# One row of attention steps for two batches: where values, sums and copies stand at its start, its middle and its end

## The chip, the cores and the metric

The kernel runs on one core of a Trainium2 chip. The metric is the device time of one launch in microseconds (us). A run's time is compared as a median over runs. One further execution of the kernel was recorded by the hardware profiler; all spans, waits and durations below come from that one execution.

## The reference: what is computed

The input x is 2 batches of 256 channels on a 56 x 56 grid, so 3136 tokens of 256 features for each batch, all in float32. Three layers follow one another:

```python
x = _L0_conv_ref(x, ...)                      # 8 groups, no softmax: f = theta^T phi / n, y = f g
t = _to_tokens(x)                             # (2, 3136, 256)
t = t + _L1_attn_ref(_ln_t(t), W_attn, W_proj)
t = t + _L1_ffn_ref(_ln_t(t), gate_w, gate_b, W1, b1, W2, b2)
x = _from_tokens(t, x)
```

The attention has 4 heads of 64 features and a causal mask:

```python
att = jnp.einsum('bhqd,bhkd->bhqk', q, k) * scale
att = jax.nn.softmax(jnp.where(causal, att, jnp.finfo(att.dtype).min), axis=-1)
y = jnp.einsum('bhqk,bhkd->bhqd', att, v)
return y.transpose(0, 2, 1, 3).reshape(B, T, C) @ W_proj
```

The last layer is a gated one: a token's two best of 8 experts (256 to 512 to 256 features, with an exact Gelu between), weighted by their softmax probabilities.

## The kernel before, in words

**Stages.** Up to about 89 us the first layer is folded into one 256 x 256 matrix a batch and applied. From 89 to about 850 us the kernel does the attention of batch 0 and then of batch 1, with the normalisation, the q, k and v products, the output projection and the routing to experts worked in between. From 850 us to the end it does the experts: 102 blocks of 128 token slots, each through `hidden` (first layer, `ht`, L1541) and `outputs` (second layer, `yp`, L1560), and adds the two expert results of each token.

**A step of attention.** `attend` (L708) is called once for each batch. It makes a list `steps`: for each block `i` of W = 448 queries (NB = 7 blocks) and each pair of heads `hp` (NH = 2 pairs), one step for every key chunk `j` of 128 keys. Within a block, whole chunks come first, and the last ones alternate with the cut ones, those that the causal mask cuts. A step has two halves:

- `scores` (L734): TensorE (PE) multiplies keys by queries into a PSUM tile `sc` (pool `psc`, two buffers), as 64x64 quarters of the array; ScalarE (ACT) takes the exponential into a tile `st` of the pool `fst` (five buffers, L753); on cut chunks VectorE (DVE) multiplies by the mask (L755). Then VectorE adds `st` into the running row `acc` (pool `fs`, two buffers): the first step of a block copies `st` into `acc` (L763), all others add (L767).
- `values` (L772): PE multiplies `st` by the values `v` into `yp` (pool `py`, one PSUM buffer). After a block's last step ScalarE copies `yp` into the buffer that `acc` was in (L796) and GpSimd (POOL) adds the two halves of it into `qT` (L797).

The main loop (L853 to L873) goes over `n`: it does `scores(n)` and `values(n - LAG)` with LAG = 3. So at the start of each call there are three scores without values, and at its end three values without scores. The order in which the code is written is the order of every engine's queue: PE, VectorE, POOL, SP and ScalarE are all under a manual schedule, and nothing moves the instructions afterwards.

**Visits.** Two steps after a block and head pair ends (BEHIND = 2) the loop calls `visit(i, hp)` (L2041) and then `sum_rows`. A visit puts other PE work between the steps: the pieces that `ahead` (L2000) names, which are transposes of normalised tokens (`xs`, PE `xp`, L600, then a ScalarE copy `px`, L606), query and key products (`qks`, L614) and value products (`vs`, L629) of the next segment of tokens, and up to two pieces of the output projection (`products`, PE `pp`, L683). POOL normalises the tokens (L585) as `xs` asks for them, one tile in advance. At the change of batch, the transposes of batch 1's first segment lie in the visit of (block 6, pair 0), and its q, k and v products and the next transposes in the visit of (block 6, pair 1), the last of batch 0's call. For batch 0 the same pieces stand ahead of the first call. In a visit PSUM tiles are taken in turn from pool `m` (two) and pool `psc` (two) by `bank` (L524) with `ring`; outside it, only from pool `m`.

`sum_rows` (L800) has PE sum `acc` over its partitions (`sp`, L809), ScalarE copy the line out (L814) and SP send it through DRAM. `invert` (four steps later) takes the reciprocal and has it spread over partitions (`rb`), `scale` (six more) multiplies the block of `qT` by it on VectorE (L841), and `hand_on` (two more) tells the projection that the block is ready. The value copy goes into `acc`'s buffer because `sum_rows` comes ahead of the block's last `values`, whose step is one later than the visit.

**The end of attention.** The last visit, of (batch 1, block 6, pair 1), loads ScalarE's table for Gelu with a one-element activation (L2045) and does one projection, `pp`. Then come the sums, the last values and, in `experts` (L1436), the register load of the experts of the first three blocks (`experts_of`, L1500), the transposes of the first block's tokens (`inputs`, PE `tp`, L1518, and a ScalarE copy `xT`, L1522), the copy of its first-layer weights by VectorE (`w`, L1529), and `hidden`. `between` (L2055) runs once a step: it issues loads of second-layer weights during the last rows and pulls other work (statistics, routing) from a queue.

The lines that make the order around the change:

```python
                LAG, BEHIND = 3, 2
                for n in range(len(steps) + LAG):
                    if BEHIND < n <= len(steps) + BEHIND and steps[n - 1 - BEHIND][4]:
                        visit(i, hp)
                        sum_rows(hp, i)
```

Of the kernel before, what the change touches and what calls it, by code (L numbers as in the profile page):

```python
# [28 lines left out]
def conv_attn_moe_kernel(  # L29
# [482 lines left out]
    def layer1(nm, general):  # L512

        with ExitStack() as whole:
# [192 lines left out]

            def attend(  # L708
                b, qT, kT, v, fst, fs, psc, py, visit, between, clock, later, finished
            ):  # L710

                steps, firsts = [], {}
                for i in range(NB):
# [13 lines left out]
                    for hp in range(NH):  # L729
                        for r, j in enumerate(order):  # L730
                            steps.append((i, hp, j, r == 0, r == len(order) - 1, order))
                sts, accs, yps = {}, {}, {}

                def scores(n):  # L734
                    i, hp, j, first, last, order = steps[n]
# [25 lines left out]
                    if first:  # L761
                        acc = fs.tile([P, 2, W], F32, tag="acc", name=f"acc_{sn}")
                        nc.vector.tensor_copy(acc, st)  # L763
                        accs[hp, i] = acc
                    else:
                        acc = accs[hp, i]
                        nc.vector.tensor_tensor(  # L767
                            acc[:k, :, c0:], acc[:k, :, c0:], st[:k, :, c0:], ALU.add
                        )
                    sts[n] = st  # L770

                def values(n):  # L772
                    i, hp, j, first, last, order = steps[n]
# [4 lines left out]
                    if first:  # L778
                        yps[hp, i] = py.tile([P, 2, 512], F32, tag="y", name=f"yp_{sn}")
                    yp = yps[hp, i]  # L780
# [11 lines left out]
                    if last:  # L792

                        yh = qT[:, hp, i * W : (i + 1) * W]
                        both = accs.pop((hp, i))
                        nc.scalar.copy(both, yp[:, :, :W])  # L796
                        nc.gpsimd.tensor_tensor(yh, both[:, 0], both[:, 1], ALU.add)  # L797
                        del yps[hp, i]

                def sum_rows(hp, i):  # L800
# [3 lines left out]
                    acc = accs[hp, i]  # L804
# [18 lines left out]
                    later.append((clock[0] + 4, invert, hp, i, yh))  # L823

                def invert(hp, i, yh):
# [12 lines left out]
                    later.append((clock[0] + 6, lambda hp, i, yh: scale(hp, i, yh, rb), hp, i, yh))  # L838

                def scale(hp, i, yh, rb):  # L840
                    nc.vector.tensor_tensor(yh, yh, rb, ALU.mult)  # L841
                    later.append((clock[0] + 2, hand_on, hp, i, yh))

                def hand_on(hp, i, yh):
                    finished[hp] = (i + 1) * W

                def due(now):
                    while later and (now is None or later[0][0] <= now):
                        _, task, hp, i, yh = later.pop(0)
                        task(hp, i, yh)  # L850
                        later.sort(key=lambda e: e[0])

                ends = {i: max(n for n, s in enumerate(steps) if s[0] == i) for i in range(NB)}  # L853
                LAG, BEHIND = 3, 2
                for n in range(len(steps) + LAG):
                    if BEHIND < n <= len(steps) + BEHIND and steps[n - 1 - BEHIND][4]:
                        i, hp = steps[n - 1 - BEHIND][:2]
                        visit(i, hp)
                        sum_rows(hp, i)
                    if n < len(steps):  # L860
                        i = steps[n][0]
                        between(i, ends[i] - n, (steps[n][2] + 1) * P > i * W + 1)

                    late = n >= LAG and steps[n - LAG][3]
# [7 lines left out]
                    if late:  # L872
                        values(n - LAG)  # L873
                return due
# [560 lines left out]

            def experts(w1s, w2s, b2s, ex, es, ps6, between, need, written, settle, decide):  # L1436
# [63 lines left out]
                def experts_of(r):  # L1500

                    b = 0 if (r + 1) * GB <= FULL0 else 1
                    s = r * GB - known[b][0]
                    return nc.values_load_multi_w_load_instructions(
                        eblks[b][0:1, s : s + GB],
# [821 lines left out]
```

## Time and profile before

| | |
|---|---|
| runs: median (lowest to highest) of 3 | 1278.05 us (1276.01 to 1281.41) |
| the profiled execution, its own time | 1279.51 us |
| its span in the trace | 1277.8 us |
| mean granted TensorE clock | 0.998 |
| L767, VectorE's adds into `acc` | x372, 373.1 us busy |
| L753, ScalarE's exponentials | x400, 330.4 us busy |
| L785 and L745, PE's values and scores | 337.3 and 335.9 us busy |
| L763, VectorE's copies into `acc` | x28, 18.0 us busy |

The table's lower half is from the profile's list of the costliest groups. Busy time is the time in which an engine had an instruction of the group in flight. The idle time in front of a row, and the instruction named with an arrow, say what the engine waited for last. In a timeline, a row is a run of like instructions: its start from the start of the span, its length, the engine, the line, the operation, and how many. Rows of PE overlap by a little, since matmuls are pipelined and their ends are modelled, so distances are best taken from start to start. "The chain" is the path of work that ended last, followed back from the last instruction.

### The profile page before, as it was taken

To read this page: it belongs to the slowest core of one execution; us is meant where nothing else is said; L and a number is where in the kernel's file an instruction comes from. 1 tells how busy PE (TensorE), PEld (TensorE's weight loads), DVE (VectorE), ACT (ScalarE), POOL (GpSimd) and SP (SyncE) were. 2 spreads that over 40 slices of the span, in tenths; PEclk is the share of its full clock that TensorE was granted. 3 is DMA by queue.
4 is the path that set the end of the run, shared out by engine and by line. 5 is a ranking of instruction groups with operands and counts; after the bars stand their busy time and mean duration, and the time that the engine had idled before them with its cause. 6 is when DMAs were issued, how large, how long until landed. Compare 5 with 4: busy or idle time off the path is not lost.

```text
span 1277.8 us, 28550 instructions
## 1 busy us (share of the span) xinstructions
PE 1251.2 (98%) x10809; PEld 816.4 (64%) x10809; DVE 786.6 (62%) x1711; ACT 613.2 (48%) x1237; POOL 357.9 (28%) x319
## 2 busy tenths in 40 slices
PE   8999999999999999999999999999999999999998
PEld 8875545444444444545544443469889899899996
DVE  2673567666777745576677878785744443455664
ACT  0255555565556555455555655553333333344432
POOL 1103230000002204221102666100256112666651
PEclk9999999999999999999999999999999999999999
DMA  9995001000000000100000123541334333466654
GB/s 312 357 346 177 24 18 32 25 9 25 9 17 10 25 1 17 35 16 9 9 9 22 66 71 100 199 137 65 100 130 150 105 113 101 142 198 199 212 160 126
DMA packets 111073, 123.87 MB, mean 97 GB/s; under 512 B 19703, under 2 KB 100840, under 8 KB 110930
## 3 DMA queue, kind: packets, MB, share of 16 engines
q1 hardware_dynamic: 100274, 95.41, 24.2%
q0 software_dynamic: 9840, 25.67, 6.0%
q8 instruction: 89, 1.46, 0.5%
q10 hardware_dynamic: 816, 0.88, 0.2%
q14 instruction: 54, 0.44, 0.1%
HBM read 62.06 MB, written 61.05 MB: 96 GB/s over the span
## 4 chain that ended last, share of the span: by engine, by line
PE 93%; DVE 3%; issue 1%; ACT 1%; another core or an unknown queue 0%; DVEq 0%; DMA 0%; ACTq 0%
PE yp_f L785 20%; PE sc_f L745 20%; PE ht_f L1541 14%; PE yp_f L1560 13%; PE qk_f L614 7%; PE v_f L629 4%; PE pp_f L683 3%; PE cp L410 3%; PE gram L317 2%; PE tp_f L1518 2%; DVE acc_f L767 1%; PE sp_f L809 1%; PE yo_f L1787 1%; PE xp_f L600 1%; ACT st_f L753 1%
## 5 line engine op out<-in xcount | busy, mean ns | idle before, releaser
L767 DVE TENSOR_TENSOR acc_f<-acc_f,st_f 128x896 f32<-128x896 f32 (+5 forms) x372 | 373.1, 1003 | 127.2 <-ACT st_f L753 117.4
L753 ACT ACTIVATE st_f<-sc_f 128x896 f32<-128x896 f32 (+5 forms) x400 | 330.4, 838 | 203.2 <-PE sc_f L745 182.8
L785 PE MATMUL yp_f<-st_f,v_f 64*64 64x448 f32 (+6 forms) x3184 | 337.3, 500 | 3.8 <-DVE st_f L755 2.0
L745 PE MATMUL sc_f<-qT_f,kT_f 64*64 64x448 f32 (+6 forms) x3184 | 335.9, 499 | 1.5 <-ACT st_f L753 1.4
L1550 ACT ACTIVATE g_f<-ht_f,b1b 128x128 f32<-128x128 f32 x408 | 116.6, 372 | 234.0 <-PE ht_f L1541 116.0
L745 PEld LDWEIGHTS sc_f<-qT_f,kT_f 64*64 64x64 f32 x3184 | 118.9, 133 | 154.6 <-issue 139.2
L785 PEld LDWEIGHTS yp_f<-st_f,v_f 64*64 64x64 f32 x3184 | 116.5, 133 | 156.7 <-issue 126.7
L1541 PE MATMUL ht_f<-xT_f,w_f 128*128 128x128 f32 x1632 | 203.2, 276 | 7.4 <-issue 6.3
L1541 PEld LDWEIGHTS ht_f<-xT_f,w_f 128*128 128x128 f32 x1632 | 197.5, 192 | 14.4 <-issue 9.1
L1420 POOL DMA_INDIRECT x_slots<-xr_f,idx x100 | 120.5, 1205 | 146.6 <-DMA y_slots<-ys_f 62.9
L797 POOL TENSOR_TENSOR qT_f<-acc_f 128x448 f32<-128x448 f32 x28 | 32.0, 1143 | 450.1 <-ACT acc_f L796 450.1
L1529 DVE COPY w_f<-w1s_f 128x1024 f32 x102 | 72.4, 711 | 95.5 <-PE ht_f L1541 32.1
L585 POOL TENSOR_SCALAR xn_f<-t 128x256 f32<-128x256 f32 (+1 forms) x50 | 84.8, 1704 | 156.9 <-PE xp_f L600 68.6
L1581 POOL DMA_INDIRECT y_tokens<-ys_f,to_f x57 | 58.9, 1034 | 127.8 <-DVE ys_f L1570 107.7
L614 PE MATMUL qk_f<-px_f,wat 128*128 128x512 f32 (+2 forms) x224 | 88.2, 546 | 0.6 <-ACT px_f L606 0.6
L1570 DVE TENSOR_TENSOR ys_f<-yp_f,kT_f 128x128 f32<-128x128 f32 x102 | 29.5, 289 | 88.3 <-PE yp_f L1560 62.5
L614 PEld LDWEIGHTS qk_f<-px_f,wat 128*128 128x128 f32 x224 | 40.6, 190 | 45.7 <-issue 41.0
L1560 PE MATMUL yp_f<-px_f,g_f 128*128 x204 | 61.6, 383 | 1.3 <-issue 1.3
L1560 PE MATMUL yp_f<-kT_f,g_f 128*128 x204 | 61.1, 381 | 0.0
L1560 PE MATMUL yp_f<-v_f,g_f 128*128 x204 | 61.0, 381 | 0.0
L755 DVE TENSOR_TENSOR st_f<-st_f,keep 128x256 f32<-128x256 f32 (+1 forms) x112 | 44.9, 401 | 26.2 <-ACT st_f L753 25.6
L1560 PE MATMUL yp_f<-w2s_f,g_f 128*128 x204 | 60.7, 379 | 0.0
(287 smaller groups left out, 1224.8 us busy)
## 6 DMA issues: line engine op xcount, KB each, us to landing
x_slots<-fill SPq DMA_DIRECT2D x1, 8190.0 KB
xb_f<-x_slots SPq DMA_DIRECT2D x60, 130.0 KB
x_slots<-fill SPq DMA_DIRECT2D x1, 7296.0 KB
y_slots<-ys_f SPq DMA_DIRECT2D x57, 128.0 KB
kept<-t SPq DMA_DIRECT2D x2, 3200.0 KB
x<-in_x_dram SPq DMA_DIRECT2D x14, 448.0 KB
rb_f<-inverses SPq DMA_DIRECT2D x56, 112.0 KB
y_f<-y_tokens SPq DMA_DIRECT2D x23, 256.0 KB
```

The costliest lines, as they stand in the source:

```text
L585: nc.gpsimd.tensor_scalar(xn[:k, a], ts[b][:k, n + a, :C], ts[b][:k, n + a, MEAN : MEAN + 1], ts[b][:k, n + a, RSTD : RSTD + 1], ALU.subtr ...
L614: nc.tensor.matmul(ps[:, :w], wat[:, c, d0 : d0 + P], px[:, s % 2, c, :w], start=(c == 0), stop=(c == NH - 1),)
L745: nc.tensor.matmul(ps[h : h + HS, a, c0:W], kT[hp][rows, j * P + h : j * P + h + HS], qT[rows, hp, q0 + c0 : q0 + W], start=True, stop=True,)
L753: nc.scalar.activation(st[:k, :, c0:], ps[:k, :, c0:W], AF.Exp, scale=SCALE)
L767: nc.vector.tensor_tensor(acc[:k, :, c0:], acc[:k, :, c0:], st[:k, :, c0:], ALU.add)
L785: nc.tensor.matmul(yp[a * HS : (a + 1) * HS, h // HS, c0:W], v[hp][h : h + HS, j, a, :HS], st[h : h + HS, a, c0:], start=first, stop=bool( ...
L1420: s = nc.gpsimd.indirect_dma_start(out=xds[b], out_offset=bass.IndirectOffsetOnAxis(ap=idxs[b][:kk, k, n : n + 1], axis=0), in_=xr[:kk], i ...
L1529: nc.vector.tensor_copy(w, w1s[:, :, bass.ds(e, 1), :].rearrange("p c e h -> p c (e h)"))
L1541: nc.tensor.matmul(ht[:, k, :], w[:, c, k * P : (k + 1) * P], xT[:, c, :], start=(c == 0), stop=(c == NH - 1),)
L1550: nc.scalar.activation(g[:, k, :], ht[:, k, :], AF.Gelu, bias=b1bs[b][:, k, i : i + 1])
L1560: nc.tensor.matmul(yp[:, :C], g[:, k, :], w2s[k][:, bass.ds(e, 1), :].rearrange("p e d -> p (e d)"), start=(k == 0), stop=(k == KH - 1),)
L1581: s = nc.gpsimd.indirect_dma_start(out=y_tokens, out_offset=bass.IndirectOffsetOnAxis(ap=to[:, n % GB : n % GB + 1], axis=0), in_=ys, in_o ...
```

## The change

1. `attend` is called once. `steps` holds both batches' steps in one list, so the values of batch 0's last three steps alternate with the scores of batch 1's first ones. `open_batch(b)`, called when a batch's first step comes, puts the batch's work into the queue.
2. Visits are kept in a table by step. A first one, (0, -1, 1), at step 2 holds what stood ahead of the first call: batch 0's value products of segment 0 and transposes of segment 1. They come after two scores.
3. At the change of batch, the transposes of batch 1's segment 0 go into the visit of (batch 0, block 5, pair 1); its q, k and v products and half of the next transposes into the visit of (block 6, pair 0), which comes FREED + LAG + 1 = 8 steps after that pair's last step in place of 3; the rest into the visit of (block 6, pair 1), which now lies among batch 1's first steps.
4. The first step of a block makes no copy: its `st` is kept, and the second step adds both into `acc`. Where the second step is cut (block 0), the columns ahead of the cut are copied: four small copies.
5. Where a block's last values come ahead of its sums, their copy goes into a buffer of the exponentials (`both`, from `fst`), since `acc` is still needed. That is so for (batch 0, block 6, pair 0) and for the last block and pair of all.
6. At the end, whole and cut chunks of the last block and pair change places. The last visit is one step earlier. In it, two first blocks of expert tokens are transposed and copied into a part of `qT` (`early_input`), with the Gelu table load ahead. The sums come after all values. The register load for the first experts goes into the visit of (batch 1, block 6, pair 0).

In the order of instructions, apart from this, one load of second-layer weights stands earlier in SP's queue, and six normalisation instructions of batch 1 stand ahead of one add (L797) in POOL's queue. The experts' order is the same after the first two blocks.

The core of the diff:

```diff
-                for i in range(NB):
+                for b, i in ((b, i) for b in range(B) for i in range(NB)):
...
                     for hp in range(NH):
+                        if (b, i, hp) == (B - 1, NB - 1, NH - 1):
+                            for r in range(len(order) - 2 * (nk - len(whole_js)), len(order), 2):
+                                order = order[:r] + [order[r + 1], order[r]] + order[r + 2 :]
...
                     if first:
-                        acc = fs.tile([P, 2, W], F32, tag="acc", name=f"acc_{sn}")
-                        nc.vector.tensor_copy(acc, st)
-                        accs[hp, i] = acc
+                        single[b, hp, i] = st
+                    elif (b, hp, i) in single:
+                        one = single.pop((b, hp, i))
+                        acc = accs[b, hp, i] = fs.tile([P, 2, W], F32, tag="acc", name=f"acc_{sn}")
+                        nc.vector.tensor_tensor(acc[:, :, c0:], one[:, :, c0:], st[:, :, c0:], ALU.add)
+                        if c0:
+                            nc.vector.tensor_copy(acc[:, :, :c0], one[:, :, :c0])
...
-                        both = accs.pop((hp, i))
+                        both = accs[b, hp, i]
+                        if (b, hp, i) not in summed:
+                            both = fst.tile([P, 2, W], F32, tag="st", name=f"both_{sn}")
                         nc.scalar.copy(both, yp[:, :, :W])
...
-                LAG, BEHIND = 3, 2
+                LAG, BEHIND, FREED = 3, 2, 4
+                visits = {BEHIND: (0, -1, NH - 1)}
+                for n, s in enumerate(steps):
+                    if s[5]:
+                        change = s[0] + 1 < B and s[1:3] == (NB - 1, 0)
+                        visits[n + 1 + (FREED + LAG if change else BEHIND)] = s[:3]
+                final = visits.pop(len(steps) + BEHIND)
+                visits[len(steps) + 1] = final
                 for n in range(len(steps) + LAG):
...
+                    if n in visits:
+                        visit(*visits[n])
+                        b, i, hp = visits[n]
+                        if i >= 0 and visits[n] != final:
+                            sum_rows(b, hp, i)
...
+                sum_rows(final[0], final[2], final[1])
                 return due
...
+            def early_input(n, qT):
+
+                tp = bank(f"first_{n}")
+                for c in range(NH):
+                    nc.tensor.transpose(
+                        tp[:, c * P : (c + 1) * P], early_rows[n][:, c * P : (c + 1) * P], ident
+                    )
+                xT = qT[:, :, n * P : (n + 1) * P]
+                nc.scalar.copy(xT, tp[:, : NH * P].rearrange("p (c t) -> p c t", c=NH))
+                early_xT.append(xT)
...
                 def ahead(b, i, hp):
...
+                    if i < 0:
+                        return vs(0), xs(1)
                     if i + 1 < NS:
                         if hp == 0:
                             return qks(i + 1), xs(i + 2)[:1]
-                        return vs(i + 1), xs(i + 2)[1:]
+                        after = projections[b + 1][0](0) if i + 2 == NS and b + 1 < B else []
+                        return vs(i + 1), xs(i + 2)[1:] + after
                     if b + 1 == B:
                         return [], []
                     xs, qks, vs = projections[b + 1]
                     if hp == 0:
-                        return [], xs(0)
-                    return qks(0) + vs(0), xs(1)
+                        return qks(0) + vs(0), xs(1)[:1]
+                    return [], xs(1)[1:]
...
+                    last = b + 1 == B and i + 1 == NB
+                    if last and hp == 0:
+                        assert ranked[0]
+                        early_ids.extend(experts_of(0))
+                    if last and hp + 1 == NH:
                         nc.scalar.activation(warm, eps5[:1], AF.Gelu)
+                        while len(early_rows) < 2:
+                            pull(every=True)
+                        now = [partial(early_input, n, qT) for n in range(2)]
                     ring.append(0)
```

## The prediction, made before the changed kernel had run

> **What bounds the kernel now.** I read the page's busy list and chain first, to find the engine that sets the end; then busy time by stage, to see where that engine has room left; then what it waits for inside the attention; then its order of time at each place that the change touches.
>
> ```profile
> PE 1251.2 (98%) x10809; PEld 816.4 (64%) x10809; DVE 786.6 (62%) x1711; ACT 613.2 (48%) x1237; POOL 357.9 (28%) x319
> PE 93%; DVE 3%; issue 1%; ACT 1%; another core or an unknown queue 0%; DVEq 0%; DMA 0%; ACTq 0%
> ```
>
> TensorE is busy for 98% of the span and is 93% of the chain that ended last. No other engine comes near, so the change can only win what TensorE loses while it waits. The stage table (start:end, length, then busy time of PE, PEld, DVE, ACT, POOL) says how much that is; the stages are attention of batch 0, attention of batch 1, and the experts:
>
> ```profile
> 89.00:463.00 374.00, 371.63 (x3635) 179.53 (x3638) 244.26 (x370) 215.83 (x327) 61.25 (x42) 1.00 0.13 39
> 463.00:852.00 389.00, 383.81 (x3718) 184.96 (x3711) 274.73 (x507) 217.30 (x327) 118.64 (x82) 1.00 0.17 52
> 852.00:1278.00 426.00, 410.08 (x2794) 378.21 (x2792) 218.48 (x673) 157.82 (x536) 168.06 (x160) 0.99 0.45 139
> ```
>
> PE is idle for 374.00 − 371.63 = 2.4 us and 389.00 − 383.81 = 5.2 us in the two attention stages, 7.6 us together: a ceiling near 0.6% of the kernel, before drains, which count as busy. The granted clock is 1.00, so there is no throttle to win from. What PE waits for between 89 and 852 us (total, times, longest):
>
> ```profile
> PE yp_f L785 <- DVE st_f L755: 2.0, 5, 0.8
> PE yp_f L785 <- ACT acc_f L796: 1.8, 3, 0.6
> PE sc_f L745 <- ACT st_f L753: 1.4, 3, 0.6
> PE ht_f L1541 <- ACT xT_f L1522: 0.8, 1, 0.8
> PE qk_f L614 <- ACT px_f L606: 0.6, 1, 0.6
> PE sp_f L809 <- ACT px_f L606: 0.5, 2, 0.2
> PE sp_f L809 <- DVE acc_f L767: 0.3, 1, 0.3
> ```
>
> These few waits sit at the start of each batch, where scores have no values to alternate with, and at the hand-over to the experts. PE at the batch change (start, length, work, idle before and releaser):
>
> ```profile
> 476.06 0.59 PE L809 MATMUL sp_f<-acc_f,ones 128*32 128x224 f32 x8 [0.24 <-ACT px_f L606]
> 479.45 0.94 PE L745 MATMUL sc_f<-qT_f,kT_f 64*64 64x192 f32 x16 [0.60 <-ACT st_f L753]
> 481.35 0.77 PE L785 MATMUL yp_f<-st_f,v_f 64*64 64x320 f32 x8 [0.21 <-DVE st_f L755]
> 493.20 1.52 PE L785 MATMUL yp_f<-st_f,v_f 64*64 64x448 f32 x16 [0.63 <-ACT acc_f L796]
> ```
>
> and at the end of attention, PE, then DVE, then POOL:
>
> ```profile
> 847.79 0.59 PE L809 MATMUL sp_f<-acc_f,ones 128*32 128x224 f32 x8 [0.27 <-DVE acc_f L767]
> 849.22 0.66 PE L1518 MATMUL tp_f<-ident,xb_f_first 128*128 128x128 f32 x4
> 850.63 2.05 PE L1541 MATMUL ht_f<-xT_f,w_f 128*128 128x128 f32 x16 [0.76 <-ACT xT_f L1522]
> ```
>
> ```profile
> 849.36 1.29 DVE L1529 COPY w_f<-w1s_f 128x1024 f32 x2 [1.28 <-PE yp_f L785]
> ```
>
> ```profile
> 850.38 1.26 POOL L797 TENSOR_TENSOR qT_f<-acc_f 128x448 f32<-128x448 f32 x1 [34.59 <-ACT acc_f L796]
> ```
>
> **What the Trainium skill says.** "TensorE: Matmul & The Clock Gate", section "Step-by-step: what each phase is for": matmuls stay in program order, and the drain of one hides beside the next but not where it stands alone. The trace agrees: where the timeline shows 0.27 us idle ahead of the sums at 847.79, more is lost (the four pp matmuls at 846.37 are 0.94 us of work, and 1.42 pass). I therefore price joints start to start, not by the idle figure. "ScalarE: Activation LUTs", section "What ACT_TABLE_LOAD costs", gives about 1283 ns for the load; the load for Gelu took 1.28 us at 846.63. "Runtime: NRT & Kernel Launch", section "Instruction fetch mechanics", says that instruction refills are mostly hidden, and that a register load is about 200 ns. This trace shows no idle time at the experts' register loads in front of 849.22 and of 852.74, but 7.6 us of "issue" stalls on PE in the experts (6.3 over 12 first-layer and 1.3 over 2 second-layer groups), which nothing else in the profile releases.
>
> **Part 1: the first steps of batch 0.** Now four v blocks, two transposes (xp), four scores, then values and scores by turns. Changed: two scores first, then v and xp, then the rest; no work is added. From the start of v at 99.74 to that of the next qk at 110.89 (both from the chain, in time) is 11.15 us. The work, each at its rate between neighbours (eight records of 64x448 0.75, 320 0.54, 192 0.33, 64 0.11; 16 v records 3.76; eight transposes 0.88): 3.76 + 0.88 + scores 0.75 + 0.54 + 0.33 + 0.11 + values 0.75 + 0.54 + 0.33 and scores of the next half 0.75 + 0.54 = 9.28. Lost: 1.87. It goes because ScalarE's exponentials of the two scores (0.92 + 0.70) and VectorE's masks (0.42 each) now lie beside 4.64 us of v and xp; v only needs transposed input, ready before. Gain **1.8**. ScalarE's queue: the two exponentials stand ahead of eight v copies of 0.27, 1.6 us late at most; with four banks v can go on, so 0.1 is left as a loss.
>
> **Part 2: the batch change.** From 464.32 (qk) to 483.84 (next qk) 19.52 us pass. Work: qk 7.06 + v 3.76 + xp 0.88 + sums 0.52 + last values 0.75 + four scores 1.73 + three values 1.62 + two scores 1.29 = 17.61. Lost 1.91. The visit at 425.06 loses 0.30 more (5.46 us for 5.16). Changed: batch 1's first scores follow batch 0's last in the same loop, so they have values to alternate with; qk and v of batch 1 move forward to the earlier visit, which itself is five steps later, when the overwritten keys are read out. They cost the same 10.82 there, and ScalarE has 4 x 0.585 + 8 x 0.27 = 4.5 us of copies beside it. What is late next: PSUM for values has one buffer, so batch 1's first values wait for ScalarE's copy out of batch 0's last (0.905 us), as they do at every block: waits of 0.58 at 120.20 and 0.63 at 493.20. Here less than two scores stand between, so 0.6 to 0.75 stays. Queued behind that values instruction on PE are all later scores. Gain 2.21 − 0.7 = **1.5**. The value copy moves to an exponentials' buffer (one of five) and is held for copy plus POOL's add, 0.905 + 1.14; the buffer's next turn is five steps on, over 7 us, so nothing. On POOL six normalisation instructions of batch 1 (1.56 each: four took 6.24 us at 392.89) pass ahead of one add at 391.76. POOL is idle for 31.32 us before that add and four of the six wait for nothing on PE, so they run there; two wait for a transpose and make the add up to 3.1 us late. It is needed by a scaling ten steps (15 us) on: nothing; without that cover, 3.1 on VectorE's queue. The two waits of the sums for px (0.24) go as well: the sums' bank no longer is one that px is being copied from.
>
> **Part 3: the end.** From 844.60 (score) to 852.90 (second first-layer group) 8.30 us pass for 6.21 of work: 2.09 lost. Changed: the whole and cut key blocks of the last row swap places, the two first expert blocks are transposed before the last projection, values come before the sums. ScalarE's xT copies and the table load (1.28 + warm 0.20) then lie under 0.94 of pp and 0.75 of values, and the sums wait for no add. Late next, first: VectorE's copy of the first weights (0.69 each; two take 1.29) may start only when the last values are read, as now at 849.36, and only the sums (0.52) cover it: 0.3 stays with the hand-over. Next: the second weights lie over the memory of the new value copy, so they wait for ScalarE 0.905, POOL 1.14 to 1.26, then 0.69 of their own, 2.8 with nothing between, against 0.52 + 0.3 + 1.78 + 0.22 = 2.8 on PE: 0.25 with hand-overs. Behind that waiting copy on VectorE stand the routing operations and later weights, not needed for 2 us. About 0.4 of drains stays. Gain 2.09 − 0.95 = **1.15**. The register load for the first block's experts goes into an earlier visit: no idle now, so nothing; if it shows there, the skill's price is 0.2 a register, two engines: up to 0.4 lost. One load of second-layer weights on SP's queue goes earlier; these land by 856 and are first used at 858.75: nothing, and if late, the 2.7 us of slack is its size.
>
> **Part 4: the copies.** 28 copies of 0.642 (18.0 us, line L763) go from VectorE, and four of 256 elements come, under 0.425 each, which an add of that size takes: 16.3 us off VectorE at 62%. The first exponentials stay in their buffer one step longer, of five: nothing. What of it is PE's? PE's waits for VectorE are the five of L755, 2.0 us. Two are the 0.2 ones of parts 1 and 2. The other three, at 529.91, 660.69 and 765.14, lose 1.01, 0.45 and 0.61 start to start, 2.07 in all. In front of them I find a queue of statistics, scalings by rb and routing work, not a copy, so I give **0.2**; bounds 0 and 2.07.
>
> **Sum.** 1.8 + 1.5 + 1.15 + 0.2 = 4.65, taken as 4.6. The profiled execution took 1279.51 with a span of 1277.8 (1.7 outside); it would take 1274.9, the span 1273.2. It stands 1.5 above the median of the runs, 1278.05, which gives 1273.4, −0.36%. About 0.5% (6.4 us) is what a measurement of this kernel can tell from no change.
>
> **Rivals.**
> A, the relief reaches further: the copies stood in the same VectorE queue all along, so the backlog at the three stalls of batch 1 is shorter by 0.64 a block, and the 2.07 goes whole, with a little of ScalarE's late starts. For: VectorE is 274.73 of 389.00 there. Against: none of the three has a copy in front. 6.7 gained: 1271.4.
> B, new waits take the place of the old: the one values buffer at the batch change and the POOL chain at the end each cost one more us or so. For: both rest on one more hand-over; against: both were counted. 2.3 gained: 1275.7.
> C, slower: instruction supply. The stream of each engine is shifted and the experts' stalls (7.6 us, of no visible cause) depend on where refills meet DMA peaks (share 0.45 there). If they double, −4.6 + 7.6 = +3.0: 1281.1. It decides from 4.6 us of new stalls. Against: the experts' order is the same.
> The change not doing what it says is hardly open: the order of instructions on the five engines shows the moves as told.
>
> **Chances.** Main case 0.50 (1272 to 1275), A 0.27, B 0.14, C 0.09. Faster by over 0.5% needs under 1271.66: more than half of A and a little of the main case, 0.30. Slower by over 0.5% (above 1284.4): the upper part of C, 0.04. The rest, 0.66, lies within. Range: from A with the late ScalarE starts, 1269.0, to B with the register load and drains, and the lower edge of C, 1279.0.
>
> **What would show it.** Right: next qk after the start comes 9.4 us after v plus two scores; no L753 wait at the batch change, one values wait there of 0.6 to 0.75; first-layer group two at about 1.15 + 3.3 us earlier than 852.90; L763 only four times; the three stalls in batch 1 still there. Wrong: those stalls gone (A); a wait over 1 us at the values after the change, or at the second first-layer group (B); "issue" stalls above 7.6 us in the experts (C).

## The result, and the profile after

The changed kernel takes 1275.2 us (median of 10 runs, 1269.95 to 1278.06); the kernel before took 1278.38 us (median of 10, 1274.22 to 1281.56). The ratio of the runs is 0.9963, with a 95% interval of 0.9950 to 0.9976: 0.37% faster, or 4.7 us by the ratio (3.2 by the medians alone). The forecast was 0.36%. The same kernel was measured twice more in the experiments, on two chips: 0.9954 (0.9940 to 0.9969) and 0.9957 (0.9943 to 0.9971).

The profile of the changed kernel, its busy list and chain first:

```profile
PE 1250.1 (98%) x10809; PEld 817.6 (64%) x10809; DVE 771.6 (61%) x1687; ACT 612.8 (48%) x1237; POOL 355.2 (28%) x319
PE 95%; DVE 2%; issue 1%; ACT 1%; DMA 0%; DVEq 0%; SPq 0%; ACTq 0%
```

VectorE has 24 instructions and 15.0 us less (16.3 were forecast). TensorE's busy time is the same within 1.1 us, and its share of the chain rises from 93 to 95%: what changed is when it waits. The stages:

```profile
89.00:463.00 374.00, 372.77 (x3554) 183.17 (x3556) 229.39 (x353) 214.24 (x333) 63.13 (x44) 1.00 0.13 39
463.00:849.00 386.00, 381.79 (x3798) 183.26 (x3790) 274.45 (x500) 218.19 (x322) 113.81 (x80) 1.00 0.17 54
849.00:1275.20 426.20, 410.10 (x2794) 378.48 (x2792) 219.30 (x676) 158.13 (x536) 168.22 (x161) 0.99 0.44 138
```

The second stage is cut at 849 in place of 852, since the second first-layer group begins that much earlier. TensorE's waits up to there:

```profile
PE yp_f L788 <- ACT acc_f L801: 2.3, 4, 0.6
PE yp_f L788 <- DVE st_f L754: 1.5, 3, 0.8
PE qk_f L614 <- ACT px_f L606: 0.6, 1, 0.6
PE sc_f L744 <- ACT st_f L752: 0.6, 1, 0.6
PE ht_f L1573 <- DVE w_f L1561: 0.3, 1, 0.3
```

The two waits on masks of 0.2, the waits of the sums and the 0.8 on `xT` are gone; the waits of values for ScalarE's copy went from three to four. The start of batch 0 on TensorE, before and then changed:

```profile
106.51 0.94 PE L745 MATMUL sc_f<-qT_f,kT_f 64*64 64x192 f32 x16 [0.50 <-ACT st_f L753]
108.44 0.77 PE L785 MATMUL yp_f<-st_f,v_f 64*64 64x320 f32 x8 [0.22 <-DVE st_f L755]
```

```profile
106.36 0.67 PE L744 MATMUL sc_f<-qT_f,kT_f 64*64 64x192 f32 x16
106.86 1.47 PE L788 MATMUL yp_f<-st_f,v_f 64*64 64x448 f32 x16
```

The waits on the exponential and on the mask are gone. The batch change, changed:

```profile
475.88 0.59 PE L815 MATMUL sp_f<-acc_f,ones 128*32 128x224 f32 x8
477.20 0.62 PE L744 MATMUL sc_f<-qT_f,kT_f 64*64 64x192 f32 x16
478.40 1.52 PE L788 MATMUL yp_f<-st_f,v_f 64*64 64x448 f32 x16 [0.59 <-ACT acc_f L801]
490.86 1.52 PE L788 MATMUL yp_f<-st_f,v_f 64*64 64x448 f32 x16 [0.58 <-ACT acc_f L801]
```

The sums and the scores come without a wait; at 478.40 stands the new one, for the single values buffer. The end on TensorE, on VectorE and on POOL:

```profile
844.31 0.66 PE L1471 MATMUL first_f<-ident,xb_f_first 128*128 128x128 f32 x4
846.80 0.58 PE L815 MATMUL sp_f<-acc_f,ones 128*32 128x224 f32 x8
847.67 2.05 PE L1573 MATMUL ht_f<-qT_f,w_f 128*128 128x128 f32 x16 [0.28 <-DVE w_f L1561]
849.86 2.05 PE L1573 MATMUL ht_f<-qT_f,w_f 128*128 128x128 f32 x16
```

```profile
846.92 0.69 DVE L1561 COPY w_f<-w1s_f 128x1024 f32 x1 [0.51 <-PE yp_f L788]
849.11 0.69 DVE L1561 COPY w_f<-w1s_f 128x1024 f32 x1 [1.50 <-POOL qT_f L802]
```

```profile
847.95 1.13 POOL L802 TENSOR_TENSOR qT_f<-both_f 128x448 f32<-128x448 f32 x1 [33.96 <-ACT both_f L801]
```

The first weights are copied once the last values are read, and the first group waits 0.28 for them. The second copy waits for POOL's add, which began when ScalarE's value copy was done.

**Where the time went.** I cut each span at the same five instructions, start to start: *start*, from the first v product or score after q and k to the next q and k; *change*, from there to the q and k products that follow batch 1's first scores; *inside*, from there to the last score but one; *end*, from there to the third first-layer group; *experts*, the rest. (The last score but one is the 64x64 one in the old order of the last row and the full one in the new; ahead of either, the same scores and values are done.)

| kernel | start | change | inside | end | experts |
|---|---|---|---|---|---|
| before | 11.24 | 372.95 | 360.30 | 10.67 | 423.06 |
| changed | 9.59 | 371.60 | 360.79 | 9.71 | 423.23 |
| e1, start undone | 10.74 | 371.61 | 358.20 | 9.71 | 406.97 |
| e2, copies back | 9.59 | 371.60 | 358.68 | 9.71 | 406.91 |
| e3, drained | 9.58 | 372.69 | 358.21 | 9.70 | 407.05 |
| e4, end undone | 9.59 | 371.60 | 358.20 | 10.68 | 407.87 |
| e5, changed again | 9.59 | 371.60 | 358.97 | 9.71 | 417.55 |
| e6, before without copies | 10.74 | 372.40 | 359.68 | 10.67 | 419.07 |
| e9, changed, third | 9.59 | 371.60 | 359.20 | 9.71 | 422.22 |
| e11, register load late | 9.59 | 371.60 | 361.00 | 9.88 | 419.22 |
| e12, value copy in acc | 9.59 | 371.61 | 359.03 | 9.51 | 421.51 |

In e7, e8 and e10 some steps pass these cuts, so they are compared over the longer stretches given with them.

Where a joint is built alike, the first two columns and the fourth repeat to 0.01 us, while whole executions of one kernel differ by several us. So the joints are read from the profiles, and the ratios below only bear out the sum. The changed kernel wins 1.65 at the start, 1.35 at the change and 0.96 at the end: 3.96 us. In this one pair of profiles 0.49 is lost inside and 0.17 in the experts, and the joints begin 0.70 later; the last section looks at how far these three are chance.

### The profile page after: what moved, and what is told of

Same layout as the page of the kernel before. It is cut to its first block, busy times and chain, and to the rows that moved or that the text cites. A ratio compares the mean times of both kernels' runs of the same rounds, so it can differ in the third digit from the quotient of the medians.

```text
span 1275.2 us, 28500 instructions
## 1 busy us (share of the span) xinstructions
PE 1250.1 (98%) x10809; PEld 817.6 (64%) x10809; DVE 771.6 (61%) x1687; ACT 612.8 (48%) x1237; POOL 355.2 (28%) x319
## 4 chain that ended last, share of the span: by engine, by line
PE 95%; DVE 2%; issue 1%; ACT 1%; DMA 0%; DVEq 0%; SPq 0%; ACTq 0%
PE yp_f L788 21%; PE sc_f L744 20%; PE ht_f L1573 14%; PE yp_f L1592 14%; PE qk_f L614 7%; PE v_f L629 4%; PE pp_f L683 4%; PE cp L410 3%; PE gram L317 2%; PE tp_f L1550 2%; PE sp_f L815 1%; DVE acc_f L770 1%; PE xp_f L600 1%; PE yo_f L1819 1%; PE tail_f L1684 0%
## 5 line engine op out<-in xcount | busy, mean ns | idle before, releaser
L752 ACT ACTIVATE st_f<-sc_f 128x896 f32<-128x896 f32 (+6 forms) x400 | 330.4, 838 | 203.4 <-PE sc_f L744 185.5
L770 DVE TENSOR_TENSOR acc_f<-acc_f,st_f 128x896 f32<-128x896 f32 (+6 forms) x344 | 344.3, 1001 | 122.0 <-ACT st_f L752 112.6
L1573 PE MATMUL ht_f<-xT_f,w_f 128*128 128x128 f32 x1600 | 199.5, 276 | 7.8 <-issue 7.6
L1573 PEld LDWEIGHTS ht_f<-xT_f,w_f 128*128 128x128 f32 x1600 | 194.0, 192 | 14.7 <-issue 10.5
```

What stands on the lines that cost most here:

```text
L752: nc.scalar.activation(st[:k, :, c0:], ps[:k, :, c0:W], AF.Exp, scale=SCALE)
L770: nc.vector.tensor_tensor(acc[:k, :, c0:], acc[:k, :, c0:], st[:k, :, c0:], ALU.add)
L1573: nc.tensor.matmul(ht[:, k, :], w[:, c, k * P : (k + 1) * P], xT[:, c, :], start=(c == 0), stop=(c == NH - 1),)
```

## The experiments

Ratios are to the kernel before on the same chip, with 95% intervals. e1 to e4 shared one chip, e5 to e8 another, e9 to e12 a third. The changed kernel itself did not run beside e1 to e4, so what each of these four lost is read from the profiles. Added back to their ratios (3.3, 3.3, 2.9 and 3.4 us faster than before), the losses 1.15, 0.47, 1.09 and 0.97 put the changed kernel 3.8 to 4.4 us ahead on that chip, an estimate with 1.1 to 1.4 us to either side.

**e1: the start undone.**

```diff
-                for piece in keys[2:]:
+                for piece in keys[2:] + vs(0) + xs(1):
-                visits = {BEHIND: (0, -1, NH - 1)}
+                visits = {}
```

> The changed kernel with part 1 alone undone: batch 0's v products and transposes stand ahead of the first score again. Theory (the gain sits in the joints where TensorE waited): from the first of these instructions to the next qk about 11.2 us in place of 9.6, with the waits of 0.5 on an exponential and 0.2 on a mask back; the rest unchanged, so about 1.65 us slower than the changed kernel. Rival (VectorE's relief is what gained): this joint's length does not come back to 11.2, since the copies stay away.

Ratio 0.9974 (0.9965 to 0.9983). The start is 10.74: it lost 1.15 of the 1.65. Neither theory has that: the first wanted all of it back, and the rival is right for the 0.50 that stays away. On TensorE and on VectorE there:

```profile
106.50 0.94 PE L744 MATMUL sc_f<-qT_f,kT_f 64*64 64x192 f32 x16 [0.50 <-ACT st_f L752]
107.25 1.50 PE L788 MATMUL yp_f<-st_f,v_f 64*64 64x448 f32 x16
```

```profile
106.48 1.04 DVE L754 TENSOR_TENSOR st_f<-st_f,keep 128x256 f32<-128x256 f32 x2 [2.45 <-ACT st_f L752]
107.55 0.87 DVE L765 TENSOR_TENSOR acc_f<-st_f,st_f 128x640 f32<-128x640 f32 x1
```

The wait on the exponential is back, the one on the mask is not. VectorE masks the first two chunks one after the other. In the kernel before, a copy stood between these masks:

```profile
106.49 0.70 DVE L755 TENSOR_TENSOR st_f<-st_f,keep 128x256 f32<-128x256 f32 x1 [2.45 <-ACT st_f L753]
107.22 0.84 DVE L763 COPY acc_f<-st_f 128x896 f32<-128x896 f32 x1
107.98 0.41 DVE L755 TENSOR_TENSOR st_f<-st_f,keep 128x256 f32<-128x256 f32 x1
```

So at this start the copy had been on the path, in front of the second mask; the start is 0.50 us shorter without it.

**e2: the copies back.** The first step of a block makes `acc` and copies `st` into it, as before; all else is the changed kernel.

```diff
                     if first:
-                        single[b, hp, i] = st
-                    elif (b, hp, i) in single:
-                        one = single.pop((b, hp, i))
-                        acc = accs[b, hp, i] = fs.tile([P, 2, W], F32, tag="acc", name=f"acc_{sn}")
-                        nc.vector.tensor_tensor(acc[:, :, c0:], one[:, :, c0:], st[:, :, c0:], ALU.add)
-                        if c0:
-                            nc.vector.tensor_copy(acc[:, :, :c0], one[:, :, :c0])
+                        acc = accs[b, hp, i] = fs.tile([P, 2, W], F32, tag="acc", name=f"acc_{sn}")
+                        nc.vector.tensor_copy(acc, st)
```

> The changed kernel with part 4 alone undone: every first exponential is copied into acc again, 28 copies of 0.64 us more on VectorE (about 16 us net). Theory (copies cost nothing on the path): no TensorE wait appears in front of a block's first steps, the joints keep their lengths, and the time is within 0.5 us of the changed kernel. Rival A (the relief shortens VectorE's backlog): 1 to 2 us slower, with longer waits on L754's masks in batch 1 or longer joints.

Ratio 0.9974 (0.9963 to 0.9984). Start, change and end are as in the changed kernel to the hundredth. Inside batch 1 it is 358.68 against 358.20 and 358.21 of e1, e3 and e4 on the same chip: the copies cost 0.47 us there. Of these, 0.18 are lost at the transposes at 636.49; the same 0.18 stand in the kernel before, at 638.31, and in no profile without copies. The rest is in this one profile alone. The long wait on a mask moves little, from 0.83 in e1 to 0.94 here:

```profile
528.09 0.66 PE L783 MATMUL yp_f<-st_f,v_f 64*64 64x256 f32 x8 [0.94 <-DVE st_f L754]
```

The rival's 1 to 2 us is not there.

**e3: the pipeline drained between the batches.**

```diff
+                    if b + 1 < B and i == NB - 1:
+                        steps += [None] * 3
```

The loop skips these three steps.

> The changed kernel with three empty steps between the two batches: the last values of batch 0 and the first scores of batch 1 no longer alternate, while the q, k and v products stay where the change put them. Theory (the interleaving is what part 2 won): waits of 0.6 on an exponential and 0.2 on a mask come back at batch 1's first scores, the values wait of 0.59 goes; 0.9 us slower in all between the two qk landmarks. Rival (what part 2 won is the moved products and the banks): no slower than 0.3 us there.

Ratio 0.9977 (0.9968 to 0.9986). The change is 1.09 longer, of the 1.35 that it had won. TensorE:

```profile
475.31 0.59 PE L817 MATMUL sp_f<-acc_f,ones 128*32 128x224 f32 x8 [0.77 <-DVE acc_f L772]
478.66 0.94 PE L746 MATMUL sc_f<-qT_f,kT_f 64*64 64x192 f32 x16 [0.56 <-ACT st_f L754]
479.42 1.47 PE L790 MATMUL yp_f<-st_f,v_f 64*64 64x448 f32 x16
```

The wait on the exponential is back as expected, and the values wait went. Not expected: the sums wait 0.77 for the last add, since of the work that stood ahead of them in the kernel before only half of the transposes is left; and the mask's 0.2 stays away, as in e1. So the rival, at most 0.3, falls, but that the total comes near the theory's 0.9 is luck in part: start to start the sums lose 0.84 more than in the changed kernel, which the theory had not. The products' new places win nothing by themselves: e6 below, in the old order, takes 372.40 without copies, and e3 takes 372.69.

**e4: the end undone.** The swap of the last row, `early_input` and the later sums are taken out; the register load stays early.

```diff
-                        if (b, i, hp) == (B - 1, NB - 1, NH - 1):
-                            for r in range(len(order) - 2 * (nk - len(whole_js)), len(order), 2):
-                                order = order[:r] + [order[r + 1], order[r]] + order[r + 2 :]
...
-                final = visits.pop(len(steps) + BEHIND)
-                visits[len(steps) + 1] = final
...
-                        now = [partial(early_input, n, qT) for n in range(2)]
```

> The changed kernel with part 3 undone but for the early register load: old order of the last row, last visit and sums ahead of the last values, the first two expert blocks transposed after attention. Theory: the stretch from the last full score to the third first-layer group is about 1.0 us longer, with 0.76 of wait on xT and 0.27 on the last add back; 1.0 us slower. Rival (the table load and xT copies were hidden anyway, the end's gain is chance): within 0.3 us.

Ratio 0.9973 (0.9965 to 0.9982). The end is 10.68, 0.97 longer, and both waits are back in the list:

```profile
PE ht_f L1567 <- ACT xT_f L1548: 0.8, 1, 0.8
PE sp_f L812 <- DVE acc_f L767: 0.3, 1, 0.3
```

The kernel before, with the late register load, has 10.67: in the old order the early load wins nothing.

**e5 and e9: the changed kernel again.** No edit.

> The changed kernel unaltered, beside the kernel before on the same chip as the three that follow. In the runs e1 to e4 the experts had no issue stalls and the late exponentials of the first two profiles were absent. Theory (three joints 4.0 us, VectorE's relief some 0.3 inside batch 1): 4.3 us faster than before, ratio about 0.9966. Rival (the first profiles' difference of 2.6 is the true one): 0.998.

> The changed kernel once more, as the measure for the three runs beside it on one chip. Up to the experts it should repeat its landmarks: 9.59 us from the first score to the next qk, 371.60 to batch 1's qk, 9.71 from the last full score to the third first-layer group. Theory (the experts' stalls belong to the chip and the execution, not to the order of the kernel): the experts' length may be anywhere between 405 and 423 us. Rival (the experts' length follows the kernel's order): near the 417.6 of e5.

e5 is at 0.9954 (0.9940 to 0.9969), e9 at 0.9957 (0.9943 to 0.9971). The joints are the same to the hundredth. 0.998, which the rival of e5 gave, lies outside both intervals; the theory's 0.9966 lies inside, near their upper ends. The experts took 417.55 and 422.22 with the same instructions in the same order, so the rival of e9, that their length follows the order, falls.

**e6: the kernel before without the copies.** Part 4 alone, put into the old loop in the same form (the reverse of e2's diff).

> The kernel before with part 4 alone: no copies of the first exponentials. e1 showed the old start at 10.74 us in place of 11.24 when the copies are gone. Theory now: the copy stands in front of the masks in VectorE's queue at each batch's first steps, so each of the two starts is 0.5 shorter, with the 0.2 waits on L755 gone, and the inside of batch 1 gains 0.3 to 0.5: 1.3 us faster than before in all, ratio 0.999. Rival (copies are wholly off the path): both starts keep their lengths of 11.24 and 19.52 and the time is the same within 0.3.

Ratio 0.9987 (0.9978 to 0.9996). The start is 0.50 shorter, the change 0.55. The theory holds at these two places. The copies of batch 0 in between were worth nothing: from the start's end to the q and k products of the next batch it took 353.43 us with and without them. The 0.62 less inside is no larger than the chance delays there (last section), so it says nothing of the copies.

**e7: three visits one step later.** Products of a visit are put between a block's last values and the next block's first ones, where the values buffer makes TensorE wait.

```diff
-                        visits[n + 1 + (FREED + LAG if change else BEHIND)] = s[:3]
+                        short = s[1:3] == (0, 0) or s[:3] == (0, NB - 1, NH - 1)
+                        visits[n + 1 + (FREED + LAG if change else LAG if short else BEHIND)] = s[:3]
```

> The changed kernel with three visits one step later, those after (block 0, pair 0) of each batch and after the last block of batch 0, so that their products stand between a block's last values and the next block's first ones. Theory (the one values buffer costs 0.58 at each of these three places, and products there hide ScalarE's copy): the three waits on L801 go, 1.7 us faster than the changed kernel. Rival (the wait moves to another instruction, the score that waits for its exponential or the sums): within 0.5 us of the changed kernel, with new waits of about that size in the same places.

Ratio 0.9954 (0.9939 to 0.9970), no better than e5. From the first score to the last but one it takes 738.30 us, e5 740.16: 1.86 won, and the three waits are gone, as at the change:

```profile
477.01 0.59 PE L815 MATMUL sp_f<-acc_f,ones 128*32 128x224 f32 x8
477.53 0.34 PE L744 MATMUL sc_f<-qT_f,kT_f 64*64 64x64 f32 x8
477.69 1.47 PE L788 MATMUL yp_f<-st_f,v_f 64*64 64x448 f32 x16
```

Its experts took 420.4, 2.9 us longer than e5's. In that comparison the gain can't be seen in the time.

**e8 and e10: the later visits, with two edits at the end.** The last value copy goes into a free buffer of `acc`, and the second expert block is transposed after the last values.

```diff
-                            both = fst.tile([P, 2, W], F32, tag="st", name=f"both_{sn}")
+                            if (b, i, hp) == (B - 1, NB - 1, NH - 1):
+                                both = fs.tile([P, 2, W], F32, tag="acc", name=f"both_{sn}")
...
-                        now = [partial(early_input, n, qT) for n in range(2)]
+                        now = [partial(early_input, 0, qT)]
...
+                early_input(1, qT)
                 sum_rows(final[0], final[2], final[1])
```

> The same as the later visits, and at the end the last value copy in a free buffer of acc, which the second first-layer weights do not lie over, and the second early expert block transposed after the last values. Theory: the wait of 0.28 before the first first-layer group falls to 0.1, the second group's weights no longer wait for POOL's add and come 0.1 to 0.2 earlier: 2.0 us faster than the changed kernel, the fastest of all. Rival (POOL's chain at the end did not hold anything): only the later visits' gain.

> The kernel of e8 again. Theory: 2.2 us shorter than the changed kernel up to the third first-layer group, as in e8, and by the time too, since the experts' own length does not depend on the order ahead of them. Rival (what is won ahead is lost again in the experts, where e8 was 1.7 us longer than e5): 0 to 0.7 us.

Ratios 0.9947 (0.9933 to 0.9961) and 0.9945 (0.9928 to 0.9961). The end is 9.32 in both, 0.39 shorter, with no wait before either first group in e8:

```profile
843.05 0.59 PE L818 MATMUL sp_f<-acc_f,ones 128*32 128x224 f32 x8
843.57 2.05 PE L1578 MATMUL ht_f<-qT_f,w_f 128*128 128x128 f32 x16
845.67 1.50 PE L1578 MATMUL ht_f<-qT_f,w_f 128*128 128x128 f32 x12
```

Up to the third group e8 is 749.87 − 747.64 = 2.23 shorter than e5, as expected. e10 is only 0.62 shorter than e9, since a late exponential (below) fell into it, which cost 1.6, and not into e9. Its experts were no longer than e9's (421.0 against 422.2), so the rival's loss there did not come. By ratio this version is ahead of the changed kernel both times, by 0.0007 and 0.0012, but the intervals overlap: the best of all that ran, likely, and not shown by the time.

**e11: the register load late.** `early_ids.extend(experts_of(0))` is taken out, so the load stands ahead of the first group again.

> The changed kernel with the register load of the first experts back in its old place, ahead of the first first-layer group. Theory (a register load costs TensorE nothing that shows): the stretch from the last full score to the third first-layer group stays 9.71 us, within 0.1. Rival (its latency was on the path): 0.2 to 1.3 us longer, with idle time ahead of the first group that no semaphore explains.

Ratio 0.9963 (0.9953 to 0.9973). The first group comes 5.76 us after the last score but one, in place of 5.41, and the third is 0.17 late. That lies between the two: more than the theory's 0.1, just under the rival's 0.2. It is not an unexplained gap either: the first group waits longer for its weights, because the load stands in VectorE's queue too. TensorE, then VectorE, then its register load here and in the kernel before (shortest, median and longest of one load in ns, and its start):

```profile
847.44 0.59 PE L815 MATMUL sp_f<-acc_f,ones 128*32 128x224 f32 x8
848.66 2.05 PE L1573 MATMUL ht_f<-qT_f,w_f 128*128 128x128 f32 x16 [0.64 <-DVE w_f L1561]
```

```profile
846.63 0.41 DVE L688 TENSOR_TENSOR t<-t,pp_f 128x264 f32<-128x264 f32 x1
847.91 0.69 DVE L1561 COPY w_f<-w1s_f 128x1024 f32 x1 [0.87 <-DMA w2s_f<-in_w_dram]
```

```profile
L1459 DVEq TENSOR_LOAD <-eblk x1: 991/991/991, 846.5 to 846.5; - x1
```

```profile
L1504 DVEq TENSOR_LOAD <-eblk x1: 999/999/999, 847.6 to 847.6; - x1
```

The load of three registers took 0.99 us here and ended at 847.53; the copy, which needs them, began at 847.91, 1.49 us after the start of the last values. In the changed kernel and in e12 it begins 1.13 after them. (e12 names the same DMA as releaser, so that DMA is not what held the copy.) The Trainium skill, "Runtime: NRT & Kernel Launch", "Instruction fetch mechanics", gives some 200 ns for a register, which makes an estimate of 0.6 us for three; the trace has 0.99, and the measurement decides. In the kernel before, the same load took 1.00 us and ended at 848.58, while the weight copy waited for the last values until 849.36: so it was hidden.

**e12: only the last value copy in `acc`'s buffer.** The first edit of e8 alone.

> The changed kernel with only the last value copy moved to acc's free buffer, so that the second first-layer weights do not wait for POOL. Theory: VectorE's second weight copy starts as soon as the first is done, some 1.5 us earlier; the second first-layer group comes about 0.1 us after the first one's end in place of 0.2 to 0.3, so 0.1 to 0.2 us gained of the 0.39 that e8 won at the end. Rival (POOL's chain ended last for that group and was the whole of it): 0.3 to 0.4.

Ratio 0.9964 (0.9952 to 0.9975). Both weight copies now run in one go, as one row shows:

```profile
845.53 1.29 DVE L1564 COPY w_f<-w1s_f 128x1024 f32 x2 [0.51 <-DMA w2s_f<-in_w_dram]
```

The end is 9.51, 0.20 shorter. So POOL's chain held the second group by that much, as the theory had it; the other 0.19 of e8 is left, by difference, to the transposes put between values and sums.

## Why the prediction was right, point by point

**The sum** was 4.65: measured are 3.96 at the joints, and 0.2 (the place that two profiles share) to 0.5 (all of e2) for the copies inside, so 4.2 to 4.5. The three ratios say 4.7, 5.9 and 5.5, with intervals of 1.6 to 1.9 to either side. That 0.37% met the forecast 0.36% so closely is luck: the interval runs from 0.24 to 0.50%. It also leaves out zero, so the 0.5% that the forecast took as the least a measurement can tell was too coarse.

**Part 1**, forecast 1.8, is 1.65. 0.31 of loss remains at the start (9.59 for 9.28 of work), where 0.1 was allowed. Another 0.09 is lost just ahead of it (last section). The forecast's 11.15 us joined times of the chain; start to start it was 11.24, a loss of 1.96.

**Part 2**, forecast 1.5, is 1.35. Without the interleaving 1.09 of it is lost (e3), though in part by another wait than the one forecast. "0.6 to 0.75 stays" came true as 0.59, and e7, where products give ScalarE's copy time, has no such wait. But the forecast's "as they do at every block" was too wide: the list before has three of these waits for 28 blocks and pairs.

**Part 3**, forecast 1.15 to the second first-layer group, is 1.07 there (8.67 to 7.60 us from the last score but one) and 0.96 to the third. "0.3 stays" for the first weights: 0.28. "0.25" for the second through POOL: 0.20 by e12. The sizes met by some luck: the 8.30 us joined a start of the timeline (844.60) with one of the chain (852.90; the timeline has 852.74), so 1.93 were lost and not 2.09. **The step that failed** is the register load: "no idle now, so nothing". That is so in the old order (e4), where the later weight copy hid the load; in the new order a late load costs 0.35 at the first group and 0.17 at the third (e11), so moving it is part of the gain. Its price was off too: 0.2 an engine is the skill's figure for one register, and the load of three took 1.00 us on VectorE in the trace before.

**Part 4**, forecast 0.2 with bounds of 0 and 2.07: by itself 1.05 at the two starts (e6), which parts 1 and 2 win again by other means, so that in the changed kernel it adds 0 there and up to 0.47 inside batch 1 (e2, one profile). The terms don't add: the two waits of 0.2 on masks were counted to the joints, and one may count them only once. The two lasting stalls behind masks, 1.02 and 0.45 start to start, stand in the changed kernel with 1.03 and 0.44, and in every variant without copies with 0.97 to 1.03 and 0.44 to 0.46, so rival A, which wanted them gone, falls. The third, 0.61 at 765.14, fell to 0.12 in the changed kernel, but in e2 as well, with the copies: not theirs either.

**Rivals B and C.** B falls: its waits came with the sizes of the main case, 0.59, 0.28 and 0.20, and none is over 1 us. C's sign did appear: the changed kernel's "issue" waits in the experts sum to 8.2 us, over the 7.6 before. But the same kernel has 6.0 in e5 and 5.6 in e9, and the experts' length changes by 16 us with the chip and the execution (407 for e1 to e4, 417.6 to 423 elsewhere). C named the right place; an effect of the order is not seen there.

**The sign that missed**: the second first-layer group was to come 4.45 us earlier than before and came 2.88 earlier, since this pair of profiles also has the 0.70 and the 0.49 against it.

## What to carry to other kernels

Where one engine is busy for 98%, look for the places at which its two streams of work can't alternate: starts, changes, ends. Lay two steps ahead of work that needs nothing from them, and price each joint start to start. A wait that is hidden today, like a register load or a copy, is hidden by a certain neighbour; when the change moves that neighbour, it has to be priced again. What is worth 1 us of 1278 shows in such a joint to the hundredth, and hardly in the time.

## What the runs showed that I had not expected

The experts' length depends on the chip and the execution. TensorE's waits after 849 us in e12:

```profile
PE ht_f L1576 <- issue: 7.4, 14, 1.2
PE yo_f L1822 <- DVE y_f L1808: 1.0, 2, 0.6
PE yp_f L1595 <- issue: 0.9, 1, 0.9
```

In e1 to e4, on one chip, no wait at all is listed there. The Trainium skill, "Runtime: NRT & Kernel Launch", "Instruction fetch mechanics", has instruction refills mostly hidden; on that chip nothing in the list speaks against it, and on the others the "issue" waits of TensorE sum to 5.4 to 8.3 us. What causes them no run shows. Refills, rival C's guess, fit badly: in the ten traces with such waits, an instruction packet of the DMA was in flight during 5 of the 126. In the same way ScalarE at times began an exponential late, as in the changed kernel:

```profile
718.16 0.92 ACT L752 ACTIVATE st_f<-sc_f 128x896 f32<-128x896 f32 x1 [0.86 <-PE sc_f L744]
721.17 1.75 ACT L752 ACTIVATE st_f<-sc_f 128x896 f32<-128x896 f32 x2 [2.09 <-PE sc_f L744]
```

TensorE then lost 0.76 at 720.63, 0.25 at 725.09 and, behind the backlog that this left on VectorE, 0.63 at 727.97. The same three stand in e10 and e11 and not in e5, e9 or e12. Together with 0.75 at 771, which every profile has but those of e1 to e4, they make up 2.4 of the 2.6 us by which the changed kernel's inside (360.79) exceeds e1's (358.20). The kernel before exceeds e1 by 2.10, of which 0.50 at the third stall (765.14), 0.77 at 774.67 and 0.50 behind a late exponential at 791.76. So the 0.49 that the first pair of profiles seemed to lose inside is the difference of two such sums of delays that come and go between executions; no loss by the change is seen in it.

Of the 0.70 ahead of the start, 0.09 belongs to the change: from the last q and k products before the start it takes 3.61 us to the first score, in every profile with the scores first, and 3.52 to the first v product in the three others. The rest is there in TensorE's first products of `turned`, at 19.70 us for 19.08, ahead of all that the change moved; what causes it is open. In the other profiles with the scores first the start lies at 99.38 to 100.85, in those with v first at 99.57 to 99.74.
